# Decay attention: choosing a chunk's experts in two steps, and turning raw sums two slots after their copy

## Chip, cores and metric

The kernel runs on one core of a Trainium2 chip. The metric is the device time of one execution in microseconds (us); less is better. TensorE (PE, with its weight loads PEld), VectorE (DVE), ScalarE (ACT), GpSimd (POOL) and SyncE (SP) each work through their own queue in order.

## The reference, cut to what matters

Sixteen layers are run one after the other on 4096 tokens of 128 values; each is `x = x + layer(layernorm(x))`. The change lies in two neighbours: an attention whose scores decay with distance, and the mixture of eight experts that follows it.

```
def _L1_attn_b_ref(x, Wq, bq, Wk, bk, Wv, bv, Wo, bo, alpha):   # 16 sequences of 256, 16 heads of 8
    scores = jnp.einsum('bqhd,bkhd->bhqk', q, k) * scale
    scores = scores * jnp.exp(-alpha * lag)
    attn = jax.nn.softmax(scores, axis=-1)
    out = jnp.einsum('bhqk,bkhd->bqhd', attn, v).reshape(B, T, D)
    return out @ Wo.T + bo
...
def _L1_ffn_ref(x, gate_w, w1, w2, w3):
    logits = jnp.einsum('nc,ec->ne', xt, gate_w)
    top_vals, top_idx = jax.lax.top_k(logits, 2)
    top_w = jax.nn.softmax(top_vals, axis=-1)
    ...                                        # each token goes through its two experts, weighed by top_w
```

## The kernel before, in words

The tokens lie feature by feature (128 partitions x 4096 columns) in `x` and are worked in eight chunks of 512 columns, that is two sequences of 256 each. The decay stage is `decay` (L2925), which hands its parts to `small_stage` (L2770). There the order of all instructions is written out by hand: a loop over **slots** (L2894), one slot for each unit of work. A chunk has eight units: for each of its two sequences, the four pairs of a query half `it` and a key half `jt`. I number slots by their place in a chunk, 0 to 7, and so on around.

In slot n the loop does, in this order:

- `score(n)` (L2796): four matmuls of 128x512 into four PSUM banks. In an even slot they read `qz,k` (the halves are equal) and DVE empties the four banks by four products with the decay table `dec` ("DVE pt L531"); one ACT exponential of 128x2048 follows in the next slot (`rest`). In an odd slot they read `qx,kx`, and ACT empties the banks with four exponentials of 128x512.
- what `later` has put down as due: first the steps of the next layer (`lead`), then `join`, `turn`, `out`.
- `weigh_by_head(n - 3)` (L2829): 16 matmuls with the values `vo`. After the second unit of each query half the sums are copied from PSUM into `raw` (two buffers), by ACT for `it` 0 (slots 0 and 4) and by DVE for `it` 1 (slots 2 and 6).
- the stage's own steps for coming chunks: the norm of `x` (for chunks that the stage before has not normed already; the first five are), `project` (slot 2), `values` (slot 3, read by "DVE vo L531"), `queries` (slots 0 and 4: `qz` by DVE and ACT), and on POOL `keys_by_edge` (`kx`, 128x512) and `queries_by_edge` (`qx`, 128x1024, end of slots 2 and 6).

`turn` (L2850) transposes `raw` on PE into one bank; DVE takes the reciprocal `rd` of the sums and multiplies (`o`). `join` (L2866) transposes the two `o` of a sequence back, and ACT copies them into `ot`. `out` (L2878) multiplies by `Wo` and adds to `x`.

All these banks come from one set of six that is handed out in turn (`bank("s")`, L511): the matmul that gets a bank waits for the reader of the allocation six before.

When a chunk's `out` is done, its lead begins: the steps of `Sending.steps` (L3574), one a slot. They are three steps of the norm (centre: PE, ACT; spread: PE, ACT; scale: DVE), `compare` (L3595: gate logits on PE, then DVE compares each expert with each other, `ahead`, 128x256), `choose` (L3614: 13 DVE instructions; the first five make `both`, the next two `sel`, the last six the shares that are sent in `out`), `place` (L3642: eight small matmuls on `both`, then DVE finds the row of each token), `turn` (L3665: the chunk transposed, two ACT copies into `out`), and four steps of two indirect DMAs each on POOL's queue (`scatter`, L3674: "POOL rows"). After the stage, `table` (L3688) counts the rows, and the experts fetch them.

The linear stage also leads into a mixture of experts, but in whole chunks (`spread` false); the rope stage uses `weigh_by_head` with `group=3`.

Of the kernel before, what the change touches and what calls it, by code (L numbers as in the profile page):

```python
# [11 lines left out]
F32, BF16, I32 = mybir.dt.float32, mybir.dt.bfloat16, mybir.dt.int32  # L12
# [5 lines left out]
P = 128  # L18
B, T, C = 16, 256, 128
NT = B * T  # L20
CH = 512
# [470 lines left out]
class Net:  # L492
# [20 lines left out]
    @contextmanager  # L513
    def share(self, **banks):

        old = self.banks
        self.psum_stack.close()
        for b in (banks, old):
            self.banks = b
            self.psum = self.psum_stack.enter_context(  # L520
                self.tc.tile_pool(name="psum", bufs=1, space=bass.MemoryType.PSUM, reuse_waits="tile")
            )
            if b is banks:
                yield
                self.psum_stack.close()
# [1124 lines left out]
class Fast(Net):  # L1650
# [169 lines left out]
    def slots(self, n, *steps, last=(), every=1):  # L1820


        both = (*steps, *last)
        with self.tc.manual_schedule():
            self.logs()
            for k in range((n - 1) * every + len(both)):
                for i in (*reversed(range(len(steps))), *reversed(range(len(steps), len(both)))):
                    c, rest = divmod(k - i, every)
                    if rest == 0 and 0 <= c < n:
                        both[i](c)  # L1830
# [939 lines left out]
    def small_stage(self, w, units, steps, tiles, evict, finish=None, group=1):  # L2770
# [10 lines left out]
        with ExitStack() as st:  # L2781
            p = self.stage(st, "sm", 1)
            items = [(c, b, *u) for c in range(NCH) for b in range(2) for u in units]
            pts, po, ots, os, rests, due = {}, {}, {}, {}, {}, {}
            lead = self.lead(p, "s", spread=True)
            first = min(at for at, _ in steps) - 3 * group
            steps = [(first + i * group, lambda c, i=i: self.norm_x_step(p, c, i, "s")) for i in range(3)] + list(steps)

            def later(n, i, f, c):


                for _ in range(i):
                    n += 1 if group == 1 or n % group < group - 2 else group - n % group
                due.setdefault(n, []).append((order.index(f) if f in order else 0, f, c))
# [34 lines left out]
            def weigh_by_head(n, slot):  # L2829
                c, b, it, jt, kind = items[n]  # L2830
                vo = tiles(c, b, it, jt)[2]
                mine = [i for i, u in enumerate(units) if u[0] == it]
                first, last = n % len(units) == mine[0], n % len(units) == mine[-1]
                if first:
                    po[it] = self.bank("o")
                pt = pts.pop(n)
                for u in range(4):
                    for r in range(4):
                        nc.tensor.matmul(
                            po[it][32 * r : 32 * r + 32, u * P : u * P + P], vo[:, 4 * r + u], pt[:, r, u],  # L2840
                            start=first and u == 0, stop=last and u == 3, skip_group_check=True,
                        )
                if last:
                    raw = p.tile([P, CH], F32, tag="raw", name="raw", bufs=2)
                    self.copy_out(it, raw, po.pop(it))
                    later(slot, 1, turn, (n, raw))
                    if it:
                        later(slot, 2, join, (slot, n))

            def turn(args):  # L2850
                n, raw = args
# [14 lines left out]
            def join(args):  # L2866
                slot, n = args
                c, b, *_ = items[n]
                if b == 0:
                    ots[c] = p.tile([P, CH], F32, tag="ot", name="ot", bufs=2)  # L2870
                pt = self.bank("s")
                for it in range(2):
                    self.tr(pt[:, it * P : it * P + P], os.pop((c, b, it)))
                self.act(ots[c][:, b * T : b * T + T], pt[:, :T], AF.Copy)
                if b == 1:
                    later(slot, 3, out, (slot, c))

            def out(args):  # L2878
                slot, c = args
                pz = self.bank("s")  # L2880
                self.mm(pz, w["Wo"], ots.pop(c))
                x = self.x[:, self.chunk(c)]
                if "bo" in w:
                    self.stt(x, pz, w["bo"], x, ALU.add, ALU.add)
                else:
                    self.tt(x, x, pz, ALU.add)
                for i, f in enumerate(lead):
                    later(slot, (2 if finish else 4) + i, f, c)

            order = [None, join, turn, out]  # L2890
            with self.share(s=6, o=2), self.tc.manual_schedule():
                self.logs()
                n = first
                while n < len(items) + 3 * group or due:  # L2894
                    if 0 <= n < len(items):
                        score(n)
                    if rest := rests.pop(n - 1, None):
                        rest()
                    for _, f, c in sorted(due.pop(n, []), key=lambda d: d[0]):
                        f(c)  # L2900
                    if group == 1:
                        mine = [n - 3]
                    else:
                        mine = range(n - 2 * group + 1, n - group + 1) if n % group == group - 1 else []
                    for i in mine:
                        if 0 <= i < len(items):
                            weigh(i, n) if finish else weigh_by_head(i, n)
                    for at, f in steps:
                        c, u = divmod(n - at, many)
                        if u == 0 and 0 <= c < NCH:  # L2910
                            f(c)
                    n += 1
# [649 lines left out]
class Sending:  # L3562
# [11 lines left out]
    def steps(self, pool, bank, w=None, spread=False):  # L3574
        net, one, p, places = self.net, self.one, self.p, self.places
# [8 lines left out]
        held, norms = {}, {}  # L3584

        def norm(i):
            def run(c):
                s = net.chunk(c)
                if i == 0:
                    norms[c] = net.norm_steps(pool, x[:, s], h0[:, s], bank, square=True)  # L3590
                norms[c][i]()

            return run
# [20 lines left out]
        def choose(c):  # L3614
            lg, ahead = held[c]
            rank = p.tile([P, 4, 8], F32, tag="rank", name="rank")
            won = p.tile([P, 4, 8], F32, tag="won", name="won")
            nc.vector.tensor_reduce(rank, ahead, AX.X, ALU.add)
            nc.vector.tensor_reduce(won, ahead.rearrange("p t a b -> p t b a"), AX.X, ALU.add)
            net.tt(rank, rank, won, ALU.subtract)  # L3620
            net.tt(rank, rank, net.k["before8"][:, None, :].broadcast_to([P, 4, 8]), ALU.add)
            both = p.tile([P, 4, 8], BF16, tag="both", name="both")
            net.ts(both, rank, 1.5, ALU.is_lt)
            sel = p.tile([P, 2, 4, 8], F32, tag="sel", name="sel")
            net.ts(sel[:, 0], rank, 0.5, ALU.is_lt)
            net.ts(sel[:, 1], rank, 1.0, ALU.is_equal)

            out = p.tile([P, 2, 4, ROW], F32, tag="out", name="out", bufs=4)
            net.tt(lg, lg, sel[:, 1], ALU.mult)
            e = p.tile([P, 4], F32, tag="e", name="e")  # L3630
            nc.vector.tensor_reduce(e, lg, AX.X, ALU.add)
            g1 = p.tile([P, 4], F32, tag="g1", name="g1")
            net.ts(g1, e, 1.0, ALU.add)
            nc.vector.reciprocal(out[:, 0, :, C + 1], g1)
            net.tt(out[:, 1, :, C + 1], out[:, 0, :, C + 1], e, ALU.mult)
            nc.vector.tensor_scalar(
                out[:, :, :, C : C + 1].bitcast(I32)[:, :, :, 0], net.k["token"].rearrange("p (k t) -> p k t", k=2),
                float(c * CH), None, ALU.add,
            )
            held[c] = both, sel, out  # L3640
# [42 lines left out]

        every = [(k, t) for k in range(2) for t in range(4)]
        parts = [every[i : i + 2] for i in range(0, 8, 2)] if spread else [every]
        return [norm(0), norm(1), norm(2), compare, choose, place, turn, *map(scatter, parts)]

    def table(self):  # L3688
        net, one, places = self.net, self.one, self.places
# [91 lines left out]
```

## Time and profile before

| What | us |
|---|---|
| median of three runs (lowest, highest) | 4450.57 (4448.54, 4456.72) |
| the profiled execution's own time | 4424.04 |
| its span, first to last instruction | 4422.3 |
| decay stage in it | about 2293 to 2597 |
| four matmuls of a score | 1.14 |
| four DVE products of an even slot | 2.48 |
| ACT exponential 128x2048 | 1.93 |
| DVE copy of `raw`; ACT copy | 0.68; 0.60 |

Each engine is busy for part of the span: PE 90%, DVE 59%, ACT 53%, POOL 48%. A busy PE includes time in which a group of matmuls has begun and its later members wait. In the views of the trace a line gives start and length in us, the engine, the line of the code, what is written and read, and in brackets the idle time before it and what ended that.

### The profile page before, as it was taken

The page shows a single profiled execution, that of the slowest core. Times are in us where ns is not written, and L with a number is a line of the kernel's source. Part 1 is how long each engine was busy: PE and PEld are TensorE (multiplying, and loading weights), DVE is VectorE, ACT ScalarE, POOL GpSimd, SP SyncE. Part 2 cuts the span into 40 slices and gives each one's busy share as a digit, 9 for nine tenths or more (in the row PEclk, how much of TensorE's full clock was granted, in tenths as well). Part 3 has the DMA queues.
Part 4 walks back from the last instruction along what each step waited for, and adds up shares of the span by engine and source line. Part 5 has one row for each costly group of instructions (what it writes and reads, how often), then busy time and mean ns, then how long its engine had stood idle before and what let it go on. Part 6 is the DMA issues. An engine that isn't in the chain of part 4 may idle for free. (4 is left out here: it accounts for less than half of the span.)

```text
span 4422.3 us, 70823 instructions
## 1 busy us (share of the span) xinstructions
PE 3983.6 (90%) x27720; PEld 2180.9 (49%) x27720; DVE 2611.8 (59%) x4477; ACT 2365.8 (53%) x4505; POOL 2124.6 (48%) x1790
## 2 busy tenths in 40 slices
PE   7899999999899999995989979887999899899878
PEld 3455455466355445543865558543333343454323
DVE  4765576365366376455336633555888698486354
ACT  6665466444766456553347633355655544774432
POOL 4653355232455155315433334456889699321241
PEclk8999999999999999997999989998999999999979
DMA  1800000000000000002620035100000000000000
GB/s 58 331 1 1 10 1 1 9 10 1 19 1 1 1 4 1 1 1 83 192 88 11 16 116 182 42 18 16 1 1 1 3 1 1 15 2 18 6 0 20
DMA packets 70390, 142.31 MB, mean 32 GB/s; under 512 B 11006, under 2 KB 39300, under 8 KB 69920
## 3 DMA queue, kind: packets, MB, share of 16 engines
q1 hardware_dynamic: 57120, 114.46, 7.8%
q0 software_dynamic: 9568, 18.51, 1.2%
q8 instruction: 222, 3.64, 0.3%
q10 hardware_dynamic: 3360, 4.72, 0.3%
q14 instruction: 120, 0.98, 0.1%
HBM read 84.22 MB, written 55.25 MB: 32 GB/s over the span
## 5 line engine op out<-in xcount | busy, mean ns | idle before, releaser
L528 ACT ACTIVATE pt<-ps 128x512 f32<-128x512 f32 (+1 forms) x896 | 423.1, 537 | 406.6 <-PE ps L504 405.3
L504 PE MATMUL ps<-hb,w 128*128 128x512 f32 (+1 forms) x960 | 470.2, 624 | 6.3 <-issue 3.3
L531 DVE TENSOR_TENSOR t<-ps,tab 128x512 f32<-128x512 f32 x512 | 319.4, 684 | 198.2 <-ACT sq L528 194.5
L504 PE MATMUL ps<-w,hb 128*128 128x512 f32 (+2 forms) x896 | 417.7, 579 | 12.2 <-DVE t L531 9.8
L534 POOL TENSOR_TENSOR t<-t,ss 128x1024 f32<-128x1024 f32 x128 | 243.5, 1902 | 311.8 <-ACT ss L528 202.7
L534 POOL TENSOR_TENSOR t<-t,t 128x512 f32<-128x512 f32 x256 | 320.3, 1273 | 13.1 <-PE ps L504 10.1
L504 PEld LDWEIGHTS ps<-hb,w 128*128 128x128 f32 (+1 forms) x960 | 182.7, 196 | 268.2 <-issue 242.4
L504 PE MATMUL ps<-nsq,ct 128*128 128x512 f32 x368 | 211.5, 659 | 73.3 <-POOL nsq L534 54.7
L534 POOL TENSOR_TENSOR nsq<-ha 128x512 f32<-128x512 f32 x112 | 122.4, 1094 | 310.7 <-ACT ha L528 298.6
L531 DVE TENSOR_TENSOR u<-u,ps 128x512 f32<-128x512 f32 x220 | 129.3, 591 | 225.1 <-PE ps L504 168.5
L528 ACT ACTIVATE pt<-pt 128x768 f32<-128x768 f32 (+1 forms) x160 | 169.6, 1060 | 155.1 <-DVE pt L531 155.1
L2185 POOL DMA_INDIRECT back<-y,x x156 | 152.8, 979 | 196.5 <-ACT y L528 170.6
L504 PE MATMUL ps<-qkt 64*128 64x192 f32 (+1 forms) x2048 | 216.2, 326 | 11.8 <-ACT pt L528 11.8
L504 PE MATMUL ps<-u,w 128*128 128x512 f32 (+1 forms) x448 | 217.6, 609 | 8.3 <-POOL u L534 8.3
L504 PE MATMUL ps<-ot,w 128*128 128x512 f32 x448 | 211.7, 605 | 14.8 <-POOL ot L534 6.6
L504 PE MATMUL ps<-xt,w 128*128 128x256 f32 x936 | 219.1, 384 | 3.9 <-DMA w<-in_moe_x 2.8
L504 PEld LDWEIGHTS ps<-qkt 64*128 64x128 f32 x2048 | 152.9, 188 | 134.5 <-ACT qkt L528 51.5
L504 PEld LDWEIGHTS ps<-w,hb 128*128 128x128 f32 x896 | 148.9, 194 | 141.0 <-issue 109.6
L531 DVE TENSOR_TENSOR pt<-ps,w 128x384 f32<-128x384 f32 (+1 forms) x320 | 171.4, 577 | 76.0 <-PE ps L504 72.6
L528 ACT ACTIVATE u<-ps,w 128x512 f32<-128x512 f32 x160 | 107.0, 685 | 186.5 <-PE ps L504 183.9
L531 DVE TENSOR_TENSOR pt<-pt,w 128x1024 f32<-128x1024 f32 (+1 forms) x96 | 182.0, 1896 | 41.9 <-ACT pt L528 41.8
L531 DVE TENSOR_TENSOR ot<-ps,rd 128x512 f32<-128x512 f32 (+1 forms) x208 | 135.8, 653 | 116.3 <-ACT rd L528 116.3
(362 smaller groups left out, 9054.8 us busy)
## 6 DMA issues: line engine op xcount, KB each, us to landing
w<-in_moe_x SPq DMA_DIRECT2D x78, 533.0 KB, 4.3
rows<-t SPq DMA_DIRECT2D x64, 520.0 KB, 11.0
x<-rows SPq DMA_DIRECT2D x78, 130.0 KB, 2.3
w<-in_local_f SPq DMA_DIRECT2D x8, 659.5 KB, 6.5
y<-back SPq DMA_DIRECT2D x16, 256.0 KB, 2.8
y<-back ACTq DMA_DIRECT2D x16, 256.0 KB, 3.4
w<-in_local_f SPq DMA_DIRECT2D x4, 658.5 KB, 7.7
back<-y,x POOLq DMA_INDIRECT x156, 2.4
```

Source lines behind the costliest of these rows:

```text
L504: self.nc.tensor.matmul(out, lhsT, rhs, start=start, stop=stop)
L528: self.nc.scalar.activation(out, in_, func, **kw)
L531: self.nc.vector.tensor_tensor(out, a, b, op)
L534: self.nc.gpsimd.tensor_tensor(out, a, b, op)
L2185: nc.gpsimd.indirect_dma_start(views[2 * i + t], bass.IndirectOffsetOnAxis(ap=x[:, t, C : C + 1].bitcast(I32), axis=0), y[:, t], None, bou ...
```

## The change

In the decay stage (and wherever `small_stage` runs with `group` 1) `turn` comes two slots after the copy of `raw` rather than one, `join` three rather than two, `out` four rather than three, and the lead one slot later. `raw` gets a third buffer (in rope too). `choose` is cut after `sel`: its second half is a step of its own, `share`, one slot later, where the lead is spread out; elsewhere both halves run in one step as before.

```diff
+            wait = int(group == 1)
...
-                    raw = p.tile([P, CH], F32, tag="raw", name="raw", bufs=2)
+                    raw = p.tile([P, CH], F32, tag="raw", name="raw", bufs=3)
                     self.copy_out(it, raw, po.pop(it))
-                    later(slot, 1, turn, (n, raw))
+                    later(slot, 1 + wait, turn, (n, raw))
                     if it:
-                        later(slot, 2, join, (slot, n))
+                        later(slot, 2 + wait, join, (slot, n))
...
-                    later(slot, 3, out, (slot, c))
+                    later(slot, 3 + wait, out, (slot, c))
...
-                    later(slot, (2 if finish else 4) + i, f, c)
+                    later(slot, (2 if finish else 4 + wait) + i, f, c)
...
             net.ts(sel[:, 1], rank, 1.0, ALU.is_equal)
-
+            held[c] = lg, both, sel
+
+        def share(c):
+
+            lg, both, sel = held[c]
             out = p.tile([P, 2, 4, ROW], F32, tag="out", name="out", bufs=4)
             net.tt(lg, lg, sel[:, 1], ALU.mult)
...
-        return [norm(0), norm(1), norm(2), compare, choose, place, turn, *map(scatter, parts)]
+        def chosen(c):
+            choose(c)
+            share(c)
+
+        first = [norm(0), norm(1), norm(2), compare]
+        return [*first, *([choose, share] if spread else [chosen]), place, turn, *map(scatter, parts)]
```

## Prediction

> **What bounds the kernel now.** The change touches the decay stage only, so I read that stage. Three views carry the prediction. The first is the table of busy time by stretches; each row is one chunk, cut where slot 7 begins (length, then busy time of PE, PEld, DVE, ACT, POOL, then the granted clock):
>
> ```profile
> 2382.63:2416.90 34.27, 31.99 (x383) 18.33 (x379) 23.54 (x59) 23.57 (x38) 13.98 (x12) 0.95 0.05 17
> 2416.90:2454.51 37.61, 33.69 (x387) 18.81 (x383) 24.75 (x60) 25.26 (x41) 15.33 (x13) 0.95 0.05 16
> 2454.51:2492.17 37.66, 33.62 (x387) 18.63 (x383) 24.76 (x60) 25.25 (x41) 15.04 (x13) 0.95 0.05 16
> 2492.17:2529.83 37.66, 33.63 (x386) 18.53 (x382) 24.84 (x60) 25.25 (x41) 15.06 (x13) 0.95 0.05 15
> 2529.83:2563.07 33.24, 29.25 (x370) 16.23 (x366) 22.32 (x56) 21.54 (x34) 12.97 (x13) 0.90 0.06 20
> ```
>
> No engine fills its chunk: DVE and ACT have 25 of 37.7 us, and part of PE's 33.6 is waiting. What PE needs at full clock I add up from start-to-start times of groups that wait for nothing: scores 8 x 1.07, weighing 8 x 1.0, four 512-column matmuls of the two norms 4.1, `turn` 4 x 0.53, `join` 2 x 0.37, `compare` 0.9, `place` 0.5, the lead's transposes 0.5, `values` 1.1, `project` 1.95, `out` 0.96: 29.4 us. So 8.2 us of a full chunk are waits. The timeline shows most of them in slot 3 of the third row's chunk (start, length, what, idle time before and who ended it):
>
> ```profile
> 2471.50 2.48 DVE L531 TENSOR_TENSOR pt<-ps,dec 128x512 f32<-128x512 f32 x4
> 2472.43 2.72 PE L504 MATMUL ps<-qx,kx 32*128 32x512 f32 x8
> ...
> 2475.31 0.18 DVE L538 TENSOR_SCALAR both<-rank 128x32 bf16<-128x32 f32 x1
> ...
> 2475.55 0.19 PE L504 MATMUL ps<-both,before 128*128 128x32 bf16 x1 [0.40 <-DVE both L538]
> ...
> 2476.78 0.69 DVE L639 COPY raw<-ps 128x512 f32<-128x512 f32 x1
> ...
> 2477.62 0.65 PE L508 MATMUL ps<-ct,raw 128*128 128x128 f32 x4 [1.71 <-ACT pt L528]
> ...
> 2478.19 1.94 PE L2839 MATMUL ps<-pt,vo 128*32 128x128 f32 x32
> ...
> 2480.06 1.84 PE L504 MATMUL ps<-w,ha 128*128 128x128 f32 x8
> ...
> 2481.82 1.14 PE L504 MATMUL ps<-qz,k 32*128 32x512 f32 x8
> ```
>
> Slot 3 lasts 2472.43 to 2481.82, 9.4 us, and needs 4.2. DVE is late: the products of slot 2 start at 2471.50, behind the comparison of slot 1, and each of the four scores waits for one of them (2.72 instead of 1.07: 1.65). `place` waits 0.4 for `both`. `turn` waits 1.7; the named ACT exponential had ended, what it needs is the copy of `raw`, which DVE runs from 2476.78 behind all 13 instructions of `choose`. Then the weighing and `values` run at half clock (1.94 and 1.84 instead of 1.08 and 1.1: 1.6). Together 5.35. The other waits: 0.9 in slot 0 (the norm's matmul, "POOL nsq"), 1.2 in slot 2 (`project`, "DVE ha"), 0.8 in slot 5 (scores behind the products of slot 4). 5.35 + 2.9 = 8.25, as the sum wants.
>
> **The change part by part.** It adds and removes no instruction: on each engine the same ones run in another order. The third `raw` buffer costs no time by itself; `turn` now reads a buffer two slots old while one newer is written, and in rope, where copies wait for "PE ps L2839" (their data), it frees nothing: 0.
>
> *DVE by slots.* Before, slots 1 and 2 hold 5.5 us (comparison 2.9, `rd`/`o` 0.55, norm 0.68, peaks 1.35) and 6.4 (products 2.4, choose 2.8, `raw` 0.6, `qz`): 12 us of DVE beside 7.7 us of PE work. After, the order is: slot 1 norms and peaks 2.6; slot 2 products, comparison, `rd`/`o`, `raw` 6.5; slot 3 first half of choose 1.8 and `vo` 0.6; slot 4 products, share 1.0, `rd`/`o`, `qz` 4.6; slot 5 `place` 0.9; slot 6 products, `rd`/`o`, `x`, `raw` 4.3. `turn` reads a copy a slot and a half old, so that wait goes, and so does the one for `both`, two slots earlier now.
>
> *What is late next.* I followed the four queues through one full chunk by hand, with start-to-start times of these rows (products 0.6 each, odd-slot exponentials 1.95 for four and 1.8 for the long one, a norm's pair 1.25, POOL's `qx` 2.4, a scatter DMA 1.3) and the rule of six banks. With slot 7 at 0: ACT finishes the exponentials of slot 7 and the long one of slot 6 at 5.0, and only then copies and squares the lead's centre, to 6.0; before, that step stood in slot 6, ahead of the exponentials. So PE's second norm matmul, in slot 0 now, waits **0.95**. ACT then runs nearly without a pause: norms, `raw`, `qz` to 11.9, exponentials of slot 1 to 13.9 (the scores of slot 2 wait for their banks, **0.65**), the long one, and `ot` at 16.0. The bank of `ot` is the one that `turn` in slot 2 gets: before, `join` was in an even slot with no exponential ahead of it; now it is behind 3.75 us of them. Wait **1.2**, and the weighing and `project` queue behind it on PE. In slot 5 `join` needs an `o` which DVE makes after products and share, at 27.85: **1.0**. Small rests: **0.3**. Sum 4.1 in place of 8.2: a full chunk takes 33.5.
>
> *POOL.* The eight DMAs start two slots later and now stand ahead of `qx` of slot 2: 15.4 + 2.4 = 17.8 in the same count, needed by the scores of slot 5 at 25.4, so the delay is covered. But while POOL multiplies, DVE's product of two SBUF tiles stands still:
>
> ```profile
> 2465.88 2.36 POOL L534 TENSOR_TENSOR qx<-qz,edge 128x1024 f32<-128x1024 f32 x1 [1.01 <-ACT qz L528]
> 2465.93 2.59 DVE L531 TENSOR_TENSOR ahead<-lg 128x256 f32<-128x256 f32 x1
> ...
> 2589.81 0.42 DVE L531 TENSOR_TENSOR ahead<-lg 128x256 f32<-128x256 f32 x1
> ```
>
> `ahead` takes 0.42 alone and 2.59 beside `qx`. In my count `ahead` falls at 15.8, again beside `qx`; the 2 us are in the 33.5, and `raw` still ends before it is turned. If they miss each other, up to 1 us less.
>
> *Other chunks.* The two before (34.25 and 34.27) lack the stage's own norm: the same walk gives 31.8, with 2.0 of waiting for the square. The last row's chunk has no `project` and `values` beside it: 28.7.
>
> *Tail.* After the last score everything is one chain. `turn` of the last sums now stands behind choose and share of the chunk before on DVE, where its `rd`/`o` wait, and the lead's square behind the exponentials: `out` of the last chunk at 18.1 to 19.6 after slot 7's start rather than 17.0. I take **+2.0** (bounds +1.1 and +2.6).
>
> *The clock.* In the stretch table 2474.70:2478.10 has PE busy for 1.29 of 3.40 us, and the next 3.40 us have clock 0.50; a longest single idle time of 1.7 was enough. The wait of 2.0 in slot 0 of the two earlier chunks can do the same. Price between 0 and 2 x 1.7; nearest to the row would be the whole, but in the worst placed stretch PE would be busy for 1.4, just above 1.29: I take half, **+1.7**.
>
> The Trainium skill ("TensorE: Matmul & The Clock Gate", Part 1) says that the clock halves after at least one idle window of about 3.4 us. The row shows less to be enough, so the measurement decides. By the page's rule the term would be 0 and the sum 1.7 lower.
>
> *Before the first lead* (2310 to 2348) the waits for fresh `raw` go and waits of `join` for `o` come, about 0.5 each: 0, bounds -2 and +2.
>
> **Sum:** 112.9 - 3 x 33.5 = 12.4; 68.5 - 63.6 = 4.9; 33.2 - 28.7 = 4.5; less 2.0 and 1.7: **18 us less**. The profiled execution (4424.04) would become 4406; the median of the runs shown is 26.5 above it, and I take the same difference off it: 4450.57 - 18 = **4432.5**.
>
> **Rivals.**
> 1. *Given back within 0.2%* (about 9 us, what a measurement here can tell from no change). If instructions that wait on each other cost their full lengths (0.68, 0.60, 2.05, 1.93 rather than start-to-start), ACT reaches `ot` a microsecond later and each wait above grows: I get 35.0 for a full chunk, 33.3 for the earlier two and 31.0 for the last: 7.9 + 1.9 + 2.2, less 3 for the tail: 9 less, 4441.5. For it: ACT would be busy from 1.2 to 16.0 nearly without a gap. Against: the rows show these groups closely pipelined.
> 2. *Slower: `join` behind the exponentials.* If ACT comes to `ot` late by the whole of them, `turn` in slots 2 and 6 waits 3.75 each rather than 1.2 and 0.2, PE stops, and the clock falls as it does now: 0.95 + 0.65 + 7.5 + 1.0 + 1.6 = 11.7 against 8.2, +3.5 a chunk, for six chunks 21, with the tail 23: 4473. It decides when the two waits together pass 4.1 + 1.4 = 5.5. A milder form (2.5 each) ends near +6. Against: ACT has 25.3 us of work in 33.5.
> 3. *All waits gone:* 24.6 + 13.9 + 8.9 = 47 less is the floor from PE's own work; with half of my new waits 31 less: 4420. For it: six banks may come free earlier than my count has it.
>
> That the change doesn't do what it says is ruled out by the order of the instructions: `share`, `turn` and `join` stand where the diff puts them.
>
> **How the numbers follow.** Forecast (9 to 28 less) 0.55; rival 3 (more than 28 less) 0.12; rival 1 (within 9 either way) 0.18; rival 2 0.15. Faster 0.67, same 0.18, slower 0.15. The range goes from 35 less to 6 more, 4415 to 4457: it leaves out some 0.04 below and 0.12 above.
>
> **What would show it.** Slot 3 near 3.2 us, slot 2 near 7.4, without half clock in either; scores of slot 3 no longer spread to 2.7 us; the wait of `turn` for `raw` gone from the list of waits and, in its place, waits of PE for ACT's square and for `ot`; chunks of 33.5. I am wrong if ACT is busy throughout slots 7 to 2 and PE's waits there pass 5 us, or if the clock drops in those slots in every chunk.

## The result, and the profile after

The changed kernel takes 4458.27 us (median of 20 runs, 4452.61 to 4465.43) against 4450.78 before (20 runs, 4445.1 to 4456.72): ratio 1.0017, 95% interval 1.0010 to 1.0023. It is 7.5 us slower, where I had forecast 18 less; the time lies outside of my range.

The table of busy time by stretches, of the changed kernel, one row for each chunk from slot 7 to slot 7 as in the prediction (length, busy time of PE, PEld, DVE, ACT, POOL, then the granted clock):

```profile
2390.62:2431.25 40.63, 36.16 (x383) 19.34 (x379) 23.58 (x59) 23.61 (x37) 13.85 (x12) 0.87 0.04 15
2431.25:2471.65 40.40, 38.03 (x386) 19.68 (x382) 24.38 (x60) 25.20 (x40) 15.16 (x13) 0.87 0.04 15
2471.65:2510.23 38.58, 36.21 (x387) 19.24 (x383) 24.24 (x60) 25.21 (x40) 15.17 (x13) 0.91 0.05 15
2510.23:2548.01 37.78, 34.60 (x386) 18.23 (x383) 24.14 (x60) 25.20 (x40) 15.16 (x13) 0.95 0.05 16
2548.01:2585.17 37.16, 32.52 (x370) 17.68 (x366) 20.65 (x56) 21.57 (x33) 9.76 (x10) 0.86 0.05 14
```

I had forecast 31.8 for the first row, 33.5 for the next three and 28.7 for the last. PE, DVE and ACT do nearly the same work as before in them; the clock is down to 0.86 to 0.91 in four of five.

What I had worked out for slot 3 did come true. The timeline of the changed kernel, slots 3 to 5 of the second row's chunk (start, length, what):

```profile
2456.56 0.18 DVE L538 TENSOR_SCALAR both<-rank 128x32 bf16<-128x32 f32 x1
...
2457.49 1.14 PE L504 MATMUL ps<-qx,kx 32*128 32x512 f32 x8
...
2461.73 0.66 PE L508 MATMUL ps<-ct,raw 128*128 128x128 f32 x4
...
2464.81 0.19 PE L504 MATMUL ps<-both,before 128*128 128x32 bf16 x1
```

Slot 3 lasts from 2457.49 to 2460.66, 3.17 us (forecast 3.2; before 9.4). Its scores take 1.14 instead of 2.72, `both` is ready 8 us before `place`, and `turn` waits for nothing. The loss comes earlier in the same chunk, in slots 0 to 2:

```profile
2438.88 1.08 PE L2840 MATMUL ps<-pt,vo 128*32 128x128 f32 x32
...
2439.11 1.01 POOL L3683 DMA_INDIRECT rows<-out,idx  x1 [0.16 <-issue]
...
2442.69 0.60 ACT L528 ACTIVATE raw<-ps 128x512 f32<-128x512 f32 x1 [2.79 <-PE ps L508]
...
2443.42 0.48 PE L2840 MATMUL ps<-pt,vo 128*32 128x128 f32 x5 [0.17 <-issue]
...
2444.93 4.93 PE L504 MATMUL ps<-qz,k 32*128 32x512 f32 x8 [0.30 <-issue]
...
2449.79 1.88 PE L504 MATMUL ps<-w,ha 128*128 128x8 f32 x8
```

The weighing of slot 0 (first line) ends at 2439.96 by the record. ACT's copy of its sums needs nothing else, and begins at 2442.69: late by 2.7 us. In between, POOL has begun to issue indirect DMAs (the second line is the first of six in a row, which last until 2446.7). The next weighing is recorded in pieces, with idle time that the view calls "issue". The scores of slot 2 take 4.93 us instead of 1.1, and what follows runs at half clock (the gate logits, the last line, take 1.88 instead of 1.06). Slot 2 lasts 12.6 us. I had 7.4.

The ends of matmuls are modelled in the profile, but the trace also holds the moments at which PE's semaphore rises, which is what the other engines wait for. (Where signals are late, some rises are missing from the record; there I take the next one.) I call a weighing late if the semaphore rises more than 0.35 us after the recorded end, and say that it ends inside a DMA if its recorded end falls between start and end of an indirect DMA on POOL, or within 0.1 us of them. In the decay stage of the changed kernel all 13 weighings that end inside a DMA are late (median 2.7 us), and none of the 37 others.

### The profile page after: what moved, and what is told of

Read it like the earlier page. It is cut to its first block, busy times and chain, and to the rows that moved or that the text cites. A ratio compares the mean times of both kernels' runs of the same rounds, so it can differ in the third digit from the quotient of the medians.

```text
span 4456.0 us, 70830 instructions
## 1 busy us (share of the span) xinstructions
PE 4002.8 (90%) x27720; PEld 2186.2 (49%) x27720; DVE 2606.7 (58%) x4477; ACT 2364.9 (53%) x4505; POOL 2124.3 (48%) x1790
## 5 line engine op out<-in xcount | busy, mean ns | idle before, releaser
L528 ACT ACTIVATE nrs<-ps,ct 128x512 f32<-128x512 f32 x208 | 139.9, 684 | 129.0 <-PE ps L504 121.3
```

Source lines behind the costliest of these rows:

```text
L528: self.nc.scalar.activation(out, in_, func, **kw)
```

## The experiments

I name the theories as the expectations do. Theory 1: indirect DMAs in a row on POOL's queue slow PE and ACT. Theory 2 (rival 2 of the prediction): PE's waits behind ACT's exponentials eat the gain. Theory 3: an accident of placement. Slots are counted through the stage: slot 31 is slot 7 of the chunk before the first full one.

### Before once more, paced DMAs, and the burst alone

These three ran beside a kernel before of 4452.31 us (15 runs).

> The kernel before, unchanged, for a second profile of it: its first profiled execution was 26 us quicker than its median. Every theory expects about 4450; what it tells is which stages were quicker in that first profile. If the decay stage takes about 316 us from its first `vo` to the first transposes of the experts again, the loss of the changed kernel is in that stage.

4454.76 us. This profile differs from the one that I had predicted from: the stage, from its first `vo` to the experts' first transposes, takes 330.1 us, not 316.2. And it has late weighings too: all 14 that end inside an indirect DMA (median 2.0 us), none of 41 others. The profile that I had predicted from has 15 such weighings and not one is late. The second profile of before, slot 6 (start, length, what, idle time before and who ended it):

```profile
2468.28 1.34 PE L504 MATMUL ps<-qz,k 32*128 32x512 f32 x8
...
2468.86 0.97 POOL L3678 DMA_INDIRECT rows<-out,idx  x1 [0.30 <-issue]
...
2470.43 1.89 DVE L531 TENSOR_TENSOR pt<-ps,dec 128x512 f32<-128x512 f32 x3 [2.30 <-PE ps L504]
```

The scores of slot 6 end from 2469.40 on by the record, but PE's semaphore rises only at 2470.36, and DVE's products of them, idle for 2.30 us by then, begin at 2470.43. Set side by side, instruction by instruction on ACT, the two profiles of before stay within 2 us up to 2013 us, part by 14 us from there to 2090, where the linear stage's lead issues its indirect DMAs, and by 14 us again in the decay stage; everything else differs by 2 to 3 us. In the linear stage's lead, too, PE's signals come late in the second profile, by up to 2.3 us, and in the first they don't. So the 26.5 us between the first profile and the median are no even offset. Nearly all of them arise where POOL issues indirect DMAs.

```diff
-return [*first, *(...), place, turn, *map(scatter, parts)]
+rest = [lambda c: None] * (6 if spread else 0)
+return [*first, *(...), place, turn, *rest, *map(scatter, parts)]
```

> The changed kernel, with six empty steps ahead of the four scatter steps of a lead, so that POOL has between the pairs of indirect DMAs the same products as before (two, `kx`, two, `qx`, two, `nsq`, two, `qx`) and not six or eight DMAs in a row. Theory 1 (six to eight indirect DMAs in a row slow PE and ACT): the gain of slot 3 stays, the long slots 7 to 2 go, no half clock there: about 18 us less than before, 4433 (4423 to 4443). Theory 2 (the gain is eaten by waits of PE behind ACT's exponentials, for the square and `ot`): those waits are as in the changed kernel, 4455 to 4460. Theory 3 (an accident of how instructions were placed, not the DMAs): 4450 to 4460, with crawling slots somewhere else.

4454.91 us, ratio to before 1.0002 (0.9993 to 1.0011). That is 22 us above what theory 1 expected, and 12 above its upper bound, though the loss against before is 5 us smaller than that of the changed kernel. The DMAs in a row are gone, and the chunks are even, but 37.7 us long. The timeline of the paced kernel, slots 0 to 2 of a full chunk:

```profile
2470.39 1.08 PE L2840 MATMUL ps<-pt,vo 128*32 128x128 f32 x32
...
2470.61 1.01 POOL L3683 DMA_INDIRECT rows<-out,idx  x1 [0.15 <-issue]
...
2473.51 0.60 ACT L528 ACTIVATE raw<-ps 128x512 f32<-128x512 f32 x1 [2.10 <-PE ps L504]
...
2476.68 2.29 PE L504 MATMUL ps<-qz,k 32*128 32x512 f32 x6 [0.65 <-ACT pt L528]
```

One pair of DMAs still falls on the weighing of slot 0. It ends at 2471.47, the semaphore rises at 2473.49, and ACT's copy begins at 2473.51. ACT's work is 1.4 to 2 us late from there: the exponentials of slot 1 start 2.5 us after their scores have ended, the scores of slot 2 wait for those banks, and half clock follows; slot 2 takes 11.4 us. Seven weighings end inside a DMA, seven are late. So it needs no six DMAs: one pair in the wrong place will do.

```diff
-return [norm(0), norm(1), norm(2), compare, choose, place, turn, *map(scatter, parts)]
+rest = [lambda c: None] * (2 if spread else 0)
+return [norm(0), norm(1), norm(2), compare, choose, place, turn, *rest, *map(scatter, parts)]
```

> The kernel before with two empty steps ahead of the scatter steps alone, which gives POOL's queue the order of the changed kernel (two DMAs, `nsq`, six DMAs in a row, `qx`, `kx`, `qx`) while DVE, ACT and PE keep the order of before. Theory 1: each chunk loses 4 to 6 us in slots 7 to 2 and gains nothing: 20 to 35 us more than before, 4470 to 4485. Theory 2: within 4 us of before. Theory 3: within 4 us of before, or anything.

4471.48 us, ratio 1.0041 (1.0027 to 1.0055): 19 us more, a little under the 20 that theory 1 had as its least. PE, DVE and ACT have the instructions of before in their order; only POOL's DMAs stand elsewhere. Twelve weighings end inside a DMA, and these twelve are late: seven by 1.0 to 8.2 us, the other five by only 0.36 to 0.43. The timeline of this kernel, slot 7 of the first chunk with a burst:

```profile
2394.27 0.73 PE L2839 MATMUL ps<-pt,vo 128*32 128x128 f32 x20
2394.33 0.97 POOL L3678 DMA_INDIRECT rows<-out,idx  x1 [0.30 <-issue]
...
2394.93 1.14 PE L504 MATMUL ps<-qx,kx 32*128 32x512 f32 x8
...
2400.70 0.97 POOL L3678 DMA_INDIRECT rows<-out,idx  x1 [0.30 <-issue]
2401.88 0.69 DVE L639 COPY raw<-ps 128x512 f32<-128x512 f32 x1 [6.44 <-remote]
...
2403.33 2.06 ACT L528 ACTIVATE pt<-ps 128x512 f32<-128x512 f32 x4 [8.21 <-remote]
```

DVE's copy of `raw` and ACT's exponentials come 6.9 and 7.3 us after the matmuls that they wait for are over by the record (2395.00 and 2396.07), behind six DMAs, of which the first and the last are shown. POOL's own products come later too, behind the DMAs, but in the list of waits PE waits for them only 2.5 us longer than in the second profile of before, in the whole stage, and DVE and ACT no longer than there. So this is the clearest proof that the place of the DMAs costs time on this chip, and theory 2 has no part in it. The kernel ran on no other chip.

### DMAs held back, DMAs behind the weighings, and the choice in two steps alone

These ran on another chip, beside a kernel before of 4423.95 us (15 runs, one of which took 7216.65). The same kernel is 28 us quicker here. Each chip that the record names was used once, so whether that belongs to the chip or to its state at the time can't be told; I say "chip" for short.

```diff
 def run(c):
+    if spread and c in (1, 2, 3):
+        kept.append((ks, c))
+        return
...                                    # those kept are issued with chunk 4's
```

> The changed kernel, with the 24 indirect DMAs of chunks 1, 2 and 3 held back and issued, after one another, with those of chunk 4: so no indirect DMA is issued in slots 31 to 54 (the three chunks with everything in them), and the end of the stage is loaded the more. Its time as a whole says little; what counts is the length of the quiet chunks. Theory 1, as the traces now show it (where POOL starts an indirect DMA while PE weighs, the end of that weighing, and of all that PE does after it, is signalled 1 to 4 us late): no weighing signalled late there, slot 2 at about 7.4 us and no half clock in it, quiet chunks of 33.5 us (33 to 34.5) rather than 37.2 to 40.4. Theory 2 (the waits for ACT's exponentials are enough by themselves): quiet chunks of 37 or more, slot 2 at 9 or more.

> The same with the kernel before: no indirect DMA in slots 29 to 52. Theory 1: it has late signals too, but in slots 5 to 0, not ahead of its waits in slot 3: quiet chunks of 36 to 37 us rather than 37.7, slot 3 at 9.4 as ever. So without indirect DMAs the change would be worth about 3 us a chunk. Theory 2: 37.7, as before.

Quiet chunks of the changed kernel: 35.0, 33.7 and 36.7 us. The middle one is what the prediction had (33.5), with slot 2 at 7.38; in the other two the clock halves in slot 2 (8.74 and 10.2). Quiet chunks of before: 37.7, 37.7 and 37.8, as with its DMAs. My expectation of 36 to 37 for before fell, and the three chunks of the changed kernel fit neither theory as a whole. The trace tells why: here no signal is late in either kernel (0 of 9 and 1 of 11 weighings that end inside a DMA), so taking the DMAs away takes nothing away. The totals (4438.71 and 4439.72) are those of a stage that ends with 32 DMAs in a row.

```diff
 self.copy_out(it, raw, po.pop(it))
+if pend and pend[0][0] <= slot:
+    self.gt(mark, raw[:, :1], raw[:, :1], ALU.mult)     # POOL, 128x1
+    _, f, c = pend.pop(0)                               # a pair of DMAs
+    f(c)
```

> The changed kernel, with the indirect DMAs of chunks 0 to 4 issued two by two, each pair behind a 128x1 product on POOL that reads the `raw` just copied, so that a pair begins when a weighing has ended and has some 2.5 us until the next. Theory 1: nearly no weighing is signalled late in slots 24 to 55, full chunks of 33.5 to 35 us, 12 to 20 us less than before: 4430 to 4439. Theory 2: within 5 us of the changed kernel, 4453 to 4463.

4419.94 us, ratio 0.9990 (0.9980 to 0.9999). The stage is 8.3 us shorter than in the first profile of before, but 4 to 9 us are lost behind it, in stages whose instructions are the same; I can't say by what. It could not test its theory here, as no signal is late without it either.

```diff
-wait = int(group == 1)
+wait = 0
```

> One part alone: `choose` cut in two steps (so `place`, the lead's transposes and the indirect DMAs come one slot later), `turn`, `join` and `out` as before. By both theories the wait of `turn` for `raw` in slot 3 shrinks by the 1.1 us of the six instructions of `share`, and `place` no longer waits: some 1.5 to 3 us a chunk less in slot 3. Theory 1 adds that POOL now has four DMAs in a row behind `nsq`: 2 to 3 us a chunk more in slots 0 and 1; sum within 8 us of before, 4443 to 4459. Theory 2: 8 to 15 less, 4436 to 4443.

4406.84 us, ratio 0.9962 (0.9949 to 0.9976): 17 us less, the whole of what I had forecast for both parts. Neither theory expected so much here. 19 weighings end inside a DMA, none is late. The timeline of this kernel, slots 1 to 3 of a full chunk:

```profile
2454.01 3.07 DVE L531 TENSOR_TENSOR ha<-ha,nrs 128x512 f32<-128x512 f32 x1
...
2454.15 2.37 POOL L534 TENSOR_TENSOR qx<-qz,edge 128x1024 f32<-128x1024 f32 x1
...
2457.23 1.96 PE L504 MATMUL ps<-ha,w 128*128 128x512 f32 x4 [1.32 <-DVE ha L531]
...
2462.26 0.68 DVE L639 COPY raw<-ps 128x512 f32<-128x512 f32 x1
...
2463.09 0.66 PE L508 MATMUL ps<-ct,raw 128*128 128x128 f32 x4 [1.26 <-DVE lg L531]
...
2463.68 1.94 PE L2840 MATMUL ps<-pt,vo 128*32 128x128 f32 x32
```

`turn` still waits for the copy of `raw`, which DVE ends at 2462.94 (the named `lg` is the product behind it): 1.26 us rather than 1.71. `place` stands in slot 4 now and waits for nothing. `project` waits 1.32 for DVE's product `ha`. A full chunk takes 34.9, or 36.5 where the clock halves.

### The changed kernel and its two halves, side by side

On a third chip, beside a kernel before of 4426.22 us (16 runs).

> The changed kernel once more, beside other runs. The traces now fall into two kinds: where the kernel before takes about 4450, all weighings that end inside an indirect DMA of POOL are signalled late (14 of 14, median 2.0 us); where it takes about 4424, none (0 of 15). Theory 1b (the change was worth what was predicted where signals are not late, and late signals alone eat it): beside a kernel before of 4424, 10 to 18 less (4406 to 4414), full chunks of 33.5 to 35; beside one of 4450, 3 to 10 more, as in the first result. Theory 2 (PE's waits for ACT take the gain anyway): no less than before in either.

4413.44 us, ratio 0.9969 (0.9956 to 0.9981): **12.8 us less**. The same program that was 7.5 us slower in the first result is faster here, and none of 14 weighings inside a DMA is late. The timeline of this profile, slots 0 to 2 of the same chunk as above:

```profile
2420.91 1.08 PE L2840 MATMUL ps<-pt,vo 128*32 128x128 f32 x32
...
2421.14 1.01 POOL L3683 DMA_INDIRECT rows<-out,idx  x1 [0.16 <-issue]
...
2422.06 0.60 ACT L528 ACTIVATE raw<-ps 128x512 f32<-128x512 f32 x1
...
2425.43 2.43 PE L504 MATMUL ps<-qz,k 32*128 32x512 f32 x8
...
2429.30 1.12 PE L508 MATMUL ps<-ct,raw 128*128 128x128 f32 x4 [0.45 <-ACT ot L528]
```

Instruction by instruction it is the stretch shown of the first profile after. The weighing ends at 2421.99 and the copy begins at 2422.06, beside the same DMA; the next weighing is in one piece; the scores of slot 2 take 2.43, not 4.93. The three full chunks of this profile:

```profile
2413.29:2448.31 35.02, 33.01 (x386) 17.97 (x382) 25.88 (x60) 25.33 (x40) 15.20 (x13) 0.95 0.05 17
2448.31:2482.00 33.69, 31.69 (x386) 17.10 (x382) 26.39 (x60) 25.12 (x40) 15.20 (x13) 1.00 0.06 18
2482.00:2518.50 36.50, 34.71 (x386) 18.63 (x382) 25.69 (x60) 25.33 (x40) 15.19 (x13) 0.91 0.05 16
```

> The choice in two steps alone, once more: its 17 us less were measured beside a kernel before of 4424. Beside one of 4450, theory 1b expects less of a gain, since its DMAs stand four in a row behind `nsq`: 0 to 12 less. Beside 4424: 17 less again.

4409.10 us, ratio 0.9959 (0.9945 to 0.9972): 17 less again.

```diff
-return [*first, *([choose, share] if spread else [chosen]), place, turn, *map(scatter, parts)]
+return [*first, *[chosen], place, turn, *map(scatter, parts)]
```

> The other part alone: `turn`, `join`, `out` and the lead one slot later, `choose` in one step. Slot 3 keeps the scores that wait for DVE's products less (the comparison is now in slot 2, behind them), `choose` of 13 instructions stands in slot 3, `place` waits for `both`. Beside a kernel before of 4424: chunks of 34 to 36, 5 to 15 less. Beside 4450: within 8 of before.

4414.80 us, ratio 0.9977 (0.9967 to 0.9987): 11 less. Full chunks take 34.3 each, with slot 2 at 7.38 and no half clock. Slot 3 takes 3.17 here too, so it is the later turn, with the comparison behind slot 2's products, that empties slot 3, and not the cut in `choose`, which brings it to 6.64. By the profiles of the stage, in us (what the columns leave out of a stage, 54 to 55, lies before the first lead):

| kernel (no signal late) | two earlier chunks | three full | last | tail | stage |
|---|---|---|---|---|---|
| before | 68.5 | 112.9 | 33.2 | 46.5 | 316.2 |
| choice in two steps | 62.1 | 106.3 | 30.9 | 45.4 | 299.8 |
| turned later | 68.2 | 102.9 | 29.8 | 51.3 | 306.2 |
| both (the change) | 67.0 | 105.2 | 28.6 | 49.8 | 304.7 |

The two parts don't add up. Turning later gains most in full chunks, and gives 3 to 5 us back in the tail, where all is one chain; on top of the choice in two steps it is a loss of 4 to 5 us.

```diff
-later(slot, 1 + wait, turn, (n, raw))
+more = int(group == 1 and it == 1 and b == 0)
+later(slot, 1 + more, turn, (n, raw))
```

> The choice in two steps, and of the raw sums only those that DVE copies in slot 2 turned a slot later (in slot 4, with their `join` in slot 5); the other turns, `out` and the lead as before. In the profile of the choice in two steps alone, PE still waits 1.26 us in slot 3 for that copy, and half clock follows in one chunk of three. If that wait goes and nothing comes for it: 1 to 2.5 us a chunk less than the choice in two steps alone, 5 to 12 us in all. If `join` in slot 5 waits for DVE's `o` instead (behind the products of slot 4): no difference.

4413.15 us, ratio 0.9971 (0.9960 to 0.9982). My edit missed its aim: the sums that DVE copies in slot 2 belong to the second sequence (`b` 1), and I moved those of the first, from slot 7 to slot 0. PE's wait in slot 3 is still there (1.25). So the question isn't answered; what the run shows is that turning only these sums later leaves a full chunk at 34.9 and makes the tail 4 us longer (49.3).

### Repeats on two more chips, and the best version

Seven more runs, beside kernels before of 4426.63 (15 runs) and 4423.24 (11 runs), were meant for a chip on which signals are late. They fell on two where they are not, so what they were to tell there stays open.

> The choice in two steps alone, a third time: 17 less twice, beside a kernel before of 4424 and 4426, with no weighing signalled late. Where the kernel before takes about 4450, theory 1b expects late signals behind the four DMAs in a row (two weighings of a chunk) and less of a gain, 0 to 12 less; a theory in which the late signals are an accident of one program's placement expects 17 less here too, and no late signals.

> The choice in two steps alone, beside the same. Where signals are late: weighings of slots 7 and 0 late behind four DMAs in a row, 0 to 12 less. Beside 4426: 17 to 19 less again.

4408.03 and 4408.87 us: ratios 0.9956 (0.9942 to 0.9969) and 0.9968 (0.9956 to 0.9979). With the other two, 14 to 19 us less on four chips, with no late weighing.

> The changed kernel with its DMAs put behind the weighings, again. Beside a kernel before of about 4450, theory 1b expects that in slots 24 to 55 nearly no weighing is signalled late, although the same chip signals them late in the kernel before: chunks of 33.5 to 35.5, 5 to 15 less than before. If they are late all the same, it isn't a DMA that begins inside a weighing that matters: 0 to 8 more. Beside 4424: 4 less, as measured.

4418.93 us, ratio 0.9983 (0.9974 to 0.9992): again a little better than before. The change without the guard had 0.9969 (0.9956 to 0.9981), but on another chip, and the two intervals overlap.

> The changed kernel without indirect DMAs in slots 31 to 54, again. Where signals are late, theory 1b expects quiet chunks of 33.5 to 36, and late signals only outside of them. Elsewhere: as measured, 35.0 and 33.6.

> The changed kernel without indirect DMAs in slots 31 to 54. Where signals are late: quiet chunks of 33.5 to 36 without a late weighing, late ones outside. Beside 4426: quiet chunks of 35.0 and 33.6, as measured.

4440.14 and 4437.72 us; quiet chunks of 35.0, 33.7 and 36.7 both times.

> The choice in two steps alone, with its DMAs put behind the weighings in the same way. Where signals are late: 10 to 18 less, more of a gain than the choice in two steps alone. Where they are not: 10 to 17 less, a little worse than that, since POOL's `qx` now waits for `raw` and two DMAs.

> The choice in two steps alone with its DMAs behind the weighings: 23.7 less beside a kernel before of 4426.6. Where the kernel before takes about 4450 and signals are late (theory 1b): nearly no weighing late in slots 24 to 55, since no DMA begins inside one, and 12 to 24 less. If the DMAs make signals late wherever they begin: 0 to 8 less, with late signals in those slots. Beside 4426 again: 20 to 25 less.

4402.97 and 4402.69 us: ratios 0.9943 (0.9930 to 0.9957) and 0.9953 (0.9939 to 0.9966). This is the best version, 21 to 24 us less than before. The change itself, which ran on another chip with signals in time, had 12.8 less. I had expected it a little worse than without the guard. Full chunks take 32.5, with no half clock. The timeline of this kernel, slots 2 and 3:

```profile
2452.98 0.68 DVE L531 TENSOR_TENSOR ha<-ha,nrs 128x512 f32<-128x512 f32 x1
...
2454.80 1.98 PE L504 MATMUL ps<-ha,w 128*128 128x512 f32 x4
...
2460.22 1.08 PE L2840 MATMUL ps<-pt,vo 128*32 128x128 f32 x32
```

POOL's `qx` now waits behind `raw` and two DMAs, and so it no longer runs beside DVE's product `ha`. That product takes 0.68 here and 3.07 beside `qx` in the choice in two steps alone; `project` waits 1.32 for it there and not at all here, and the weighing of slot 3 keeps its full clock (1.08 in this profile, 1.94 in the other). So, by the trace, this gain is not the one that the guard was built for; no run separates the later `qx` from the later DMAs. On a chip with late signals it wasn't measured.

## Why the prediction was wrong

The profile that I predicted from (4424.04, no late signal) looks like those of the chips on which signals are in time; the median (4450.57) and the profile after look like the other kind. The record doesn't name the chips of the first result, so this is read from times and signals. Everything in the prediction up to the sum was about signals in time, and there the direction was right: 12.8 less (0.9956 to 0.9981 is 8 to 19 less) against 18. The times that decide came from the other kind. **The step that failed** is the last one of the sum, "the median of the runs shown is 26.5 above it, and I take the same difference off it". I took the 26.5 us for an offset that both kernels share. They are, nearly all, the price of late signals, and a price that the change moves: where signals are late it came to 7.5 more instead of 12.8 less.

The stage by parts, changed kernel less before, in us:

| part | forecast | signals in time | signals late |
|---|---|---|---|
| before the first lead | 0 | -1.0 | -0.9 |
| two earlier chunks | -4.9 | -1.5 | +2.4 |
| three full chunks | -12.4 | -7.7 | +3.2 |
| last chunk | -4.5 | -4.6 | -3.4 |
| tail | +2.0 | +3.3 | +4.6 |
| clock | +1.7 | in the rows above | in the rows above |
| stage | -18 | -11.5 | +6.0 |
| whole kernel, measured | -18 | -12.8 | +7.5 |

- *POOL.* "The eight DMAs start two slots later [...] so the delay is covered" asked only when the queue gets to `qx`. In time, that holds: quiet chunks are as long as the others. Where signals are late, the DMAs cost by what PE does beside them, and the change put six to eight of them in a row beside slots 7 to 2, where before they stood in pairs between POOL's products. That moving them alone costs 19 us there, with the order of PE, DVE and ACT untouched, is shown. That their place is what costs the changed kernel its gain is argued from it, from 13 late weighings of 13, and from the same program without late signals; no kernel took the late signals away on that chip.
- *Slot 3.* Right: 9.4 to 3.17 in the full chunks of both profiles of the changed kernel. The waits of the scores, of `place` and of `turn` went, and the half clock in that slot.
- *What is late next.* The places were right and the sizes mixed. Norm's second matmul behind ACT's square: 0.77 (forecast 0.95). Scores of slot 2: 1.4 (2.43 less 1.07; 0.65). `turn` behind `ot`: 0.45 (1.2). `join` for `o`: 0.78 (1.0). Where the clock stays up, a full chunk takes 33.7 (33.5), and slot 2 takes 7.39 (7.4).
- *The clock* is the term that was mis-sized where signals are in time. I priced the wait in slot 0 of the two earlier chunks, at 1.7 in all. The clock does fall in those two, but in slot 2 (8.2 and 8.3 us), and in slot 2 of two of the three full chunks too (8.74 and 10.2 against 7.39). Against a forecast of 63.6 and 100.5, these chunks take 67.0 and 105.2: 8 us more, where I had put 1.7. In the full chunks 4.1 of it is measured, against the one that kept its clock (33.7). The two earlier chunks have no such neighbour; by estimate, a granted clock of 0.95 over 33.5 us is worth 1.7 in each, which is all of the 3.4 that they are longer. Together that is 7.5. The test that I had named, full chunks without half clock, fails.
- *Tail.* 3.3, above my upper bound of 2.6.
- *The rivals.* Rival 2 (PE behind `join` and `ot`) did not happen: that wait is 0.45, and it decided from 5.5. The first result lies where its milder form would have ended, "near +6", by another cause. None of my rivals had it. The row was there to be asked, since 26.5 us lay between two figures of the same kernel.

What stays open: what makes signals late on one chip and not on others, and whether a DMA behind a weighing leaves the next signal in time on such a chip. The kernels that would have shown it never ran on one.

## What to carry to other kernels

If the profiled execution is far from the median, find out where the difference arises before you subtract anything from either: a second profile, laid beside the first instruction by instruction, shows it in one look. A transfer that is "off the path" still has a place, and the place has a price: ask what the engines are doing at the moment when it is issued. And split a change into its parts before you keep it: here one half brought 14 to 19 us on four chips, and the other, worth 11 by itself on the chip where it was tried, took 4 to 5 of them back when it was added.

## What the runs showed of the hardware

- **Late signals.** On the chip of the first group of experiments, as in the first profile after, each weighing that ended inside an indirect DMA of POOL was signalled late: 46 of 46 in four kernels (medians 2.0 to 2.7 us, the longest 8.2), and 0 of 164 others. In the runs on the other four chips, and in the first profile of before, it was 1 of 204. PE seems to have done the work by then: in the paced kernel its semaphore stands still from 2470.47 to 2473.49 and then rises six times in 0.23 us, for matmuls that take 3 us by the record. DVE's semaphore rose on time in that stretch. The recorded end of a matmul shows none of it; the waiting engine's idle time does, and the semaphore's own times.
- The Trainium skill ("SBUF — State Buffer", section "Who interferes with whom") says that a DMA never contends with a compute engine. That is about ports into SBUF. In time, the quiet chunks agree (33.7 with the DMAs and without); where signals are late, the runs differ from what a reader would take from it, 19 us for DMAs moved and nothing else.
- **A DVE product of two SBUF tiles beside POOL's `qx`** took 3.07 us, and 0.68 away from it, as `ahead` took 2.59 and 0.42. In the kernel that has POOL's product behind it, with the DMAs, a full chunk takes 32.5 rather than 34.9.
